# Last layer, first image: the nine convolution steps of both channel halves taken in turn on DVE

## The chip, the cores and the metric

The kernel runs on one core of a Trainium2 chip. The metric is the device time of one execution in microseconds, and the figure of a kernel is the median of several executions. Engine names are those of the profile: PE multiplies matrices (PEld loads its weights), DVE, ACT and POOL do elementwise work, SP issues the DMAs of this kernel. One core has one of each. The engines run at the same time; each takes its own instructions strictly in order, and semaphores make an instruction wait for another engine or for a DMA.

## The reference, cut to what matters

Four layers follow one another on a batch of 4 images of 192 channels and 56 x 56 pixels, all float32. The first three are an attention with a 7 x 7 convolution and an MLP, a channel attention, and a windowed attention with a gated MLP. The change is in the fourth, a scan in four directions:

```python
xn = _ln_cf(x, ln_w, ln_b)                             # layer norm over the channels
xz = jnp.einsum('dc,bchw->bdhw', in_proj_w, xn)
xc, z = jnp.split(xz, 2, axis=1)                       # 192 channels each
xc = jax.lax.conv_general_dilated(xc, conv_w, (1, 1), 'SAME', feature_group_count=xc.shape[1])
xc = jax.nn.silu(xc + conv_b[None, :, None, None])     # 3 x 3, each channel by itself
...
x_dbl = jnp.einsum('kcd,bkdl->bkcl', x_proj_w, xs)     # xs: xc by rows, by columns, and both reversed
dts, Bv, Cv = jnp.split(x_dbl, [R, R + N], axis=2)
dt = jax.nn.softplus(jnp.einsum('kdr,bkrl->bkdl', dt_proj_w, dts) + dt_proj_b[None, :, :, None])
ys = _selective_scan(xs, dt, A, Bv, Cv) + Ds[None, :, :, None] * xs
...                                                    # y: the sum of the four directions
y = _ln_cf(y, out_norm_w, out_norm_b) * jax.nn.silu(z)
return x + jnp.einsum('cd,bdhw->bchw', out_proj_w, y)
```

The selective scan is a recurrence along the pixels, h = exp(dt A) h + dt B u, for 192 channels with 4 states each, and its output is the sum of C h over the states.

## The kernel before

**Tiles.** The 192 channels lie as two halves (`h` = 0, 1) of 96 partitions. An image is worked through in 7 chunks of 8 image rows, 448 pixels (`NCHUNK`, `CH`). For each image `b` and chunk `c` the generator `begin(b, c)` does the front of the layer:

- a DMA brings the chunk's rows of x into a `row` tile; POOL clears the edges of a tile `pad` and copies the two rows above from the chunk before; two `pad` tiles are used in turn;
- `layer_norm`: PE means (L1823), DVE subtracts (L1825), ACT squares (L1833), PE takes the variance (L1838), ACT Ln and Exp (L1841, L1842), DVE multiplies (L1844). L1825, L1833 and L1844 handle both halves in one instruction of 896 elements;
- PE projects the two halves of the convolution's source (L1878, in `project`) and ACT writes them into `pad` (L1889, one instruction a half);
- the 3 x 3 convolution of each half, in nine steps, from `pad` into `u`. For image 0 the steps run on DVE: a `tensor_scalar` for the first tap with the bias (L1912), eight `scalar_tensor_tensor` (L1914) that each multiply a shifted view of `pad` by a weight and add `u`. For images 1 to 3 they are nine matrix multiplications on PE with diagonal weights (L1921), made once on DVE by `diagonals` (L1958);
- PE projects the halves of z (L1878 again) and ACT copies them out (L1939, into a `gate` tile);
- ACT takes SiLU of `u` (L1944) and of z (L1945), the latter goes to memory (`zmem`), and `product` multiplies `u` by the scan's projection (PE L1975, ACT L1978, a DMA to `prods`).

The convolution handles 7 image rows in chunk 0 (392 elements a step), 8 in chunks 1 to 5 (448), 9 in chunk 6 (504), because it lags the chunk by one row.

**The scan** follows in `load` (DMAs of the projected values: `dr`, `bc`), `sizes` (PE L2067, ACT softplus L2079, into `dt`), `decay` (DMAs that spread `dt` over the states into `da`, ACT exponential L2113) and `scan`: DVE forms `du` (L2128; L2131 for columns), PE repeats it for the states (L2138), DVE multiplies by B (L2144) and scans (L2160), POOL multiplies by C (L2167), PE sums over the states (L2183), DVE adds to `y` (L2188, L2197). Two directions start on an image's rows, then come its columns.

**The order of the work.** No engine's order is written by hand as a list. All work is in generators such as `begin`; before each group of instructions a generator yields what the group costs on a planning clock. The class `Order` keeps all open generators, works out for each when its next group could start (its engine's last planned end, the end of the group it depends on plus 0.25, free buffers), takes the earliest, with a small charge for a later place in the program (`HURRY` times the place), emits its instructions, and goes on. So the order of each engine's instructions is fixed when the program is built, and it depends on the costs that the generators yield:

```python
def on_dve(*n, takes=(), ready=None, each=0.00105):
    return "DVE", sum(0.08 + each * i for i in n), takes, None, ready
```

An optional `ready` replaces the end of the group before as the earliest start. `table=` names the set of functions that an ACT group needs; where it differs from the one last used, an ACT table load is emitted (L331) and 1.3 is charged.

**What stands around.** Image 0's front of the last layer is emitted among the end of the third layer and the start of the last layer's scan. Of the third layer the steps concerned are a norm of its last chunks (PE L1249, ACT L1260, L1268, L1269, DVE L1271), its depthwise convolution on DVE (L1397 and L1399, taps outside, the parts of a tap inside the loop), and the MLP's multiplications and their elementwise work (L1488, L1499, L1523, L1553, L1562, L1570, L1580). Two large clears by POOL (L2243) stand at the start of the scan.

Of the kernel before, what the change touches and what calls it, by code (L numbers as in the profile page):

```python
# [22 lines left out]
B, C, H, W = 4, 192, 56, 56  # L23
# [204 lines left out]
def pixels(ap):  # L228

    return ap.rearrange("(h p) n -> p h n", p=HALF)  # L230
# [9 lines left out]
def rows2(ap, w=W):  # L240
    return ap.rearrange("p (y x) -> p y x", x=w)


class Order:
# [29 lines left out]
    def take(self, kind="bank"):  # L274
        slot = min((s for s in self.kinds[kind] if s[0] is not None), key=lambda s: s[0])
        slot[0] = None
        return slot[1]

    def done(self, tile):

        (slot,) = (s for slots in self.kinds.values() for s in slots if s[1] is tile)
        slot[0] = self.end + self.LATENCY
# [57 lines left out]
def on_pe(n, *takes, ready=None):  # L340

    return "PE", 0.0019 * n, takes, None, ready


def on_dve(*n, takes=(), ready=None, each=0.00105):
    return "DVE", sum(0.08 + each * i for i in n), takes, None, ready
# [6 lines left out]
def on_act(*n, takes=(), table=None, ready=None):  # L353
    return "ACT", sum(0.2 + 0.0009 * i for i in n), takes, table, ready


def on_pool(*n, each=0.0011):
    return "POOL", sum(0.2 + each * i for i in n), (), None, None


def on_sp(*takes):
    return "SP", 0.5, takes, None, None
# [1371 lines left out]
def layer3(tc, order, pools, src, packs, aps, dst):  # L1734
# [80 lines left out]
    def gone(*what):  # L1815
        return what in passed

    def layer_norm(x, out, over=(), read=None):

        yield on_pe(2 * CH, "bank")  # L1820
        mean = take()
        for k in range(2):
            nc.tensor.matmul(mean[:HALF, :CH], ones, x[:, k], start=(k == 0), stop=(k == 1))  # L1823
        yield on_dve(2 * CH)
        nc.vector.tensor_sub(out[:HALF], x[:HALF], bcast(mean[:HALF, :CH], 1, 2))  # L1825
        done(mean)
        for t in over:
            done(t)
        if read:
            passed.add(read)  # L1830
        yield on_act(2 * CH, takes=("sq3",))
        sq = take("sq3")
        nc.scalar.activation(sq[:HALF], out[:HALF], AF.Square)  # L1833
        yield on_pe(2 * CH, "bank")
        vt = take()
        var = vt[:HALF, :CH]
        for k in range(2):
            nc.tensor.matmul(var, ones, sq[:, k], start=(k == 0), stop=(k == 1))  # L1838
        done(sq)
        yield on_act(CH, CH, table=EXP_LN)  # L1840
        nc.scalar.activation(var, var, AF.Ln, bias=eps)  # L1841
        nc.scalar.activation(var, var, AF.Exp, scale=-0.5)  # L1842
        yield on_dve(2 * CH)
        nc.vector.tensor_mul(out[:HALF], out[:HALF], bcast(var, 1, 2))  # L1844
        done(vt)

    def begin(b, c):

        yield lambda: (b, c) == (0, 0) or (gone("begun", b, c - 1) if c else gone("begun", b - 1, NCHUNK - 1))
        yield lambda: b < 2 or gone("scanned", b - 2)

        yield lambda: b == 0 or gone("multiplied", 8 * NSC * (b - 1) + 4 * c)

        yield lambda: order.at2["tail"] >= NCHUNK * (b + 1)
        u = us[b % 2]
        yield on_sp("row", "row")
        xl, xn = take("row"), take("row")
        nc.sync.dma_start(xl[:HALF], pixels(src[b])[:, :, c * CH : (c + 1) * CH])  # L1860

        i = NCHUNK * b + c
        pad, above = pads[i % 2], pads[(i - 1) % 2]
        yield lambda: i < 2 or gone("convolved", i - 2)
        yield on_pool(200, 200)
        nc.gpsimd.memset(pad[:HALF, :, :, 0 : W + 2 : W + 1], 0.0)
        if c == 0:
            nc.gpsimd.memset(pad[:HALF, :, 1], 0.0)
        else:
            nc.gpsimd.tensor_copy(pad[:HALF, :, 0:2, 1 : 1 + W], above[:HALF, :, 8:10, 1 : 1 + W])  # L1870
        if c == NCHUNK - 1:
            nc.gpsimd.memset(pad[:HALF, :, 10], 0.0)
        yield from layer_norm(xl, xn, over=(xl,))

        def project(m):
            px = take()
            for k in range(2):
                nc.tensor.matmul(  # L1878
                    px[:HALF, :CH], inT[:, k, HALF * m : HALF * m + HALF], xn[:, k], start=(k == 0), stop=(k == 1)
                )  # L1880
            return px

        tiles = []
        for m in range(2):
            yield on_pe(2 * CH, "bank")
            tiles.append(project(m))
        for m in range(2):
            yield on_act(CH)
            nc.scalar.activation(  # L1889
                pad[:HALF, m, 2:10, 1 : 1 + W],  # L1890
                rows2(tiles[m][:HALF, :CH]),
                AF.Identity,
                bias=in_b[:, m : m + 1],
            )
            done(tiles[m])
        passed.add(("begun", b, c))
        y0, y1 = max(8 * c - 1, 0), 8 * c + (8 if c == NCHUNK - 1 else 7)
        n = y1 - y0
        at = y0 - (8 * c - 1)
        px = slice(y0 * W, y1 * W)  # L1900
        zt = None
        for h in range(2):
            pz = pc = uh = None
            if b == 0:

                for t in range(9):
                    yield on_dve(n * W, each=0.0012, ready=order.end - 0.3 if t else None)
                    v = pad[:HALF, h, at + t // 3 : at + t // 3 + n, t % 3 : t % 3 + W]
                    uh = rows2(u[:HALF, h, px])
                    wt = w["c96.conv_w"][:, h, t : t + 1]  # L1910
                    if t == 0:
                        nc.vector.tensor_scalar(uh, v, wt, w["c96.conv_b"][:, h : h + 1], ALU.mult, ALU.add)  # L1912
                    else:
                        nc.vector.scalar_tensor_tensor(uh, v, wt, uh, ALU.mult, ALU.add)  # L1914
            if uh is None:
                yield lambda: gone("diagonals")
            for t in range(9 if uh is None else 0):
                yield on_pe(n * W, *(("bank",) if t == 0 else ()), ready=order.end - 0.5 if t else None)
                if t == 0:
                    pc = take()  # L1920
                nc.tensor.matmul(  # L1921
                    rows2(pc[:HALF, : n * W]),
                    diag[:, h, t],
                    pad[:, h, at + t // 3 : at + t // 3 + n, t % 3 : t % 3 + W],
                    start=(t == 0),
                    stop=(t == 8),
                )
            if uh is None:
                yield on_act(n * W)
                nc.scalar.activation(  # L1930
                    u[:HALF, h, px], pc[:HALF, : n * W], AF.Identity, bias=w["c96.conv_b"][:, h : h + 1]
                )
                done(pc)
            yield on_pe(2 * CH, "bank")
            pz = project(2 + h)
            yield on_act(CH, takes=() if h else ("gate",))
            if h == 0:
                zt = take("gate")
            nc.scalar.activation(zt[:, h], pz[:HALF, :CH], AF.Identity, bias=in_b[:, 2 + h : 3 + h])  # L1939
            done(pz)  # L1940
        done(xn)
        passed.add(("convolved", i))
        yield on_act(2 * n * W, 2 * CH, table=SILU)
        nc.scalar.activation(u[:HALF, :, px], u[:HALF, :, px], AF.Silu)  # L1944
        nc.scalar.activation(zt, zt, AF.Silu)  # L1945
        yield on_sp()
        nc.sync.dma_start(pixels(zmem[b])[:, :, c * CH : (c + 1) * CH], zt)
        done(zt)
        yield from product(b, 0, px, u[:, :, px], 2)
        passed.add(("rows", b, c))  # L1950
# [16 lines left out]
    def product(b, o, px, u, passes):  # L1967

        n = px.stop - px.start
        yield on_pe(passes * n, "bank")  # L1970
        pp = take()

        out = pp[:40, :n].rearrange("p (x y) -> p y x", y=H) if o else pp[:40, :n]
        for k in range(2):
            nc.tensor.matmul(out, w["c128.xpT"][:, k, o], u[:, k], start=(k == 0), stop=(k == 1))  # L1975
        yield on_act(n, takes=("prod",))
        t = take("prod")
        nc.scalar.copy(t[:, :n], pp[:40, :n])  # L1978
        done(pp)
        yield on_sp()  # L1980
        nc.sync.dma_start(prods[b][o][:, px], t[:, :n])
        done(t)
# [227 lines left out]
    n = 8 * NSC  # L2210
# [72 lines left out]
```

## Time and profile before

| | us |
|---|---|
| median of 3 executions | 6766.48 |
| lowest to highest | 6764.02 to 6773.46 |
| the profiled execution, its own time | 6756.62 |
| its span in the profile | 6754.8 |
| busy: PE, DVE, ACT, POOL | 5757.1, 5976.0, 2615.2, 1414.7 |
| mean granted PE clock | 0.931 of full speed |
| ACT table loads, 373 of 1283 ns | 478.6 |

The profile is of one execution. Its page gives the busy time of each engine, the span in 40 equal slices (of 169 us here), the groups of instructions by line, engine and tile with their mean durations and what ended the idle time before them, and the chain of work that ended last. Queries of the trace give the same for a stretch of time: busy time by stage, and a timeline, in which one row is one instruction or a run of like instructions on one engine (start, length, engine, line, operation, output<-inputs, shapes, count, then in brackets the idle time before it and the releaser). A row's length for a run of several instructions is from the first start to the last end. The front of image 0 in the last layer lies between 4789 and about 4980 us of the span.

### The profile page before, as it was taken

The page shows a single profiled execution, that of the slowest core. Times are in us where ns is not written, and L with a number is a line of the kernel's source. Part 1 is how long each engine was busy: PE and PEld are TensorE (multiplying, and loading weights), DVE is VectorE, ACT ScalarE, POOL GpSimd, SP SyncE. Part 2 cuts the span into 40 slices and gives each one's busy share as a digit, 9 for nine tenths or more (in the row PEclk, how much of TensorE's full clock was granted, in tenths as well). Part 3 has the DMA queues.
Part 4 walks back from the last instruction along what each step waited for, and adds up shares of the span by engine and source line. Part 5 has one row for each costly group of instructions (what it writes and reads, how often), then busy time and mean ns, then how long its engine had stood idle before and what let it go on. Part 6 is the DMA issues. An engine that isn't in the chain of part 4 may idle for free.

```text
span 6754.8 us, 107251 instructions
## 1 busy us (share of the span) xinstructions
PE 5757.1 (85%) x43558; PEld 2642.5 (39%) x43558; DVE 5976.0 (88%) x7515; ACT 2615.2 (39%) x4049; POOL 1414.7 (21%) x1413
## 2 busy tenths in 40 slices
PE   6999889999999995768888788786689889889776
PEld 3444444444444442335444444453222222222211
DVE  2999999999999999838999899898888887887997
ACT  1121121222222121125555455454366566566544
POOL 0000000000000000132222222221025544545564
PEclk9999889999999997889999899998799999999998
DMA  4222112221222112210000000000045555655654
GB/s 107 59 53 59 36 30 62 52 67 34 54 56 73 30 44 75 62 42 16 18 18 16 18 19 15 18 18 22 23 113 134 150 144 131 161 134 138 171 149 118
DMA packets 252042, 462.65 MB, mean 68 GB/s; under 512 B 30388, under 2 KB 237964, under 8 KB 240412
## 3 DMA queue, kind: packets, MB, share of 16 engines
q1 hardware_dynamic: 251548, 455.80, 26.8%
q8 instruction: 343, 5.62, 0.4%
q14 instruction: 151, 1.24, 0.1%
HBM read 238.58 MB, written 62.96 MB: 45 GB/s over the span
## 4 chain that ended last, share of the span: by engine, by line
DVE 26%; PE 20%; issue 4%; ACT 4%; POOL 1%; DMA 1%; SPq 0%; DVEq 0%; POOLq 0%; ACTq 0%
DVE bg L1399 6%; PE bank L1921 4%; DVE st L2160 3%; DVE bxn L1399 3%; PE bank L1878 2%; DVE bank L2144 2%; PE bank L2138 2%; PE bank L2183 2%; PE bank L1562 1%; PE bank L1265 1%; DVE bacc L1711 1%; PE bank L2011 1%; PE bank L1249 1%; DVE e L1650 1%; PE bank L1488 1%
## 5 line engine op out<-in xcount | busy, mean ns | idle before, releaser
L811 DVE TENSOR_TENSOR pr<-vdx,attn 112x1792 f32<-112x1792 f32 (+4 forms) x720 | 1185.9, 1648 | 19.2
L656 PE MATMUL bank<-qk_in,w_a 64*49 64x392 f32 x9408 | 1157.4, 496 | 0.0
L2167 POOL TENSOR_TENSOR da<-st,bc 128x448 f32<-128x448 f32 x672 | 857.3, 1281 | 844.2 <-DVE st L2160 630.3
L816 DVE TENSOR_TENSOR oa<-oa,pr 112x1792 f32<-112x1792 f32 (+1 forms) x423 | 765.0, 1808 | 0.0
L656 PE MATMUL bank<-qk_in,wd 64*49 64x392 f32 x4032 | 691.3, 494 | 0.0
L2160 DVE TENSOR_TENSOR_SCAN st<-da,st,bank 128x448 f32<-128x448 f32 x576 | 646.8, 1132 | 0.7 <-ACT da L2113 0.7
L656 PEld LDWEIGHTS bank<-qk_in,w_a 64*49 64x49 f32 x9408 | 431.7, 120 | 396.1 <-issue 390.4
L1147 POOL MEMSET bxl<- 128x1008 f32 x3 | 2.7, 938 | 2783.3 <-DVE ob L825 2783.3
L2144 DVE TENSOR_TENSOR bank<-bank,bc 128x448 f32<-128x448 f32 x672 | 382.7, 617 | 114.6 <-PE bank L2138 114.1
L331 ACT ACT_TABLE_LOAD x373 | 478.6, 1283 | 6.7
L2113 ACT ACTIVATE da<-da,a_neg 128x448 f32<-128x448 f32 x672 | 413.8, 658 | 111.7 <-DMA da<-dt 109.6
L1399 DVE SCALAR_TENSOR_TENSOR bg<-bzpad,w_b,bg 128x448 f32<-128x448 f32 (+2 forms) x672 | 423.6, 685 | 0.0
L2183 PE MATMUL bank<-da,w_c 128*32 128x448 f32 x1344 | 355.5, 575 | 72.7 <-POOL da L2167 66.9
L816 DVE TENSOR_TENSOR ob<-ob,pr 112x1792 f32<-112x1792 f32 (+3 forms) x282 | 393.1, 1394 | 0.0
L902 ACT ACTIVATE hm<-bank,w_a 128x448 f32<-128x448 f32 x168 | 106.4, 634 | 637.3 <-PE bank L893 617.8
L2138 PE MATMUL bank<-du,w_c 32*128 32x448 f32 x1344 | 261.6, 626 | 105.0 <-DVE du L2128 62.8
L656 PEld LDWEIGHTS bank<-qk_in,wd 64*49 64x49 f32 x4032 | 247.8, 119 | 256.7 <-issue 254.8
L893 PE MATMUL bank<-xc,w_a 128*128 128x448 f32 x672 | 296.8, 571 | 58.6 <-DVE xc L878 58.6
L608 ACT ACTIVATE qk_in<-bank,qk_bias,qk_scale 64x224 f32<-64x224 f32 (+5 forms) x288 | 146.3, 526 | 445.5 <-PE bank L593 443.2
L1488 PE MATMUL bank<-bxn,w_b 128*128 128x448 f32 (+2 forms) x672 | 291.4, 562 | 22.5 <-DVE bxn L1271 17.1
L908 PE MATMUL bank<-hm,w_a 128*96 128x448 f32 x672 | 288.5, 561 | 20.2 <-ACT hm L902 20.2
L1921 PE MATMUL bank<-pad,diag 128*96 128x448 f32 (+2 forms) x756 | 297.4, 543 | 2.3 <-ACT pad L1889 2.3
(309 smaller groups left out, 9908.4 us busy)
## 6 DMA issues: line engine op xcount, KB each, us to landing
da<-dt SPq DMA_DIRECT2D x672, 224.0 KB
vdx<-vmem SPq DMA_DIRECT2D x168, 476.0 KB
bc<-prod SPq DMA_DIRECT2D x224, 224.0 KB
row<-x SPq DMA_DIRECT2D x56, 336.0 KB
x<-x SPq DMA_DIRECT2D x4, 2352.0 KB
vmem<-vt SPq DMA_DIRECT2D x56, 168.0 KB
xc<-x SPq DMA_DIRECT2D x56, 168.0 KB
mid<-xc SPq DMA_DIRECT2D x56, 168.0 KB
```

What stands on the lines that cost most here:

```text
L331: self.nc.scalar.preload_act_table_set(table)
L656: nc.tensor.matmul(py[a][outs[g], : 7 * W].rearrange("p (y x) -> p y x", x=W), wt[halves[a], dx], q[halves[a], r, i0 + m : i0 + m + 7, dx ...
L811: nc.vector.tensor_mul(pr, vv, wt)
L816: nc.vector.tensor_add(og, og, before)
L1399: nc.vector.scalar_tensor_tensor(dst, x, wt[:, t : t + 1], dst, ALU.mult, ALU.add)
L1921: nc.tensor.matmul(rows2(pc[:HALF, : n * W]), diag[:, h, t], pad[:, h, at + t // 3 : at + t // 3 + n, t % 3 : t % 3 + W], start=(t == 0), ...
L2113: nc.scalar.activation(da, da, AF.Exp, scale=a_neg[:, k, g : g + 1])
L2138: nc.tensor.matmul(tiles[j][:, :SCH], w["c96.rep"][r], du[r], start=True, stop=True)
L2144: nc.vector.tensor_mul(tiles[j][:, :SCH], tiles[j][:, :SCH], b_)
L2160: nc.vector.tensor_tensor_scan(sts[j][:, r], da[:, r], tiles[j][:, :SCH][:, r], first, ALU.mult, ALU.add)
L2167: nc.gpsimd.tensor_mul(da, sts[j], c_)
L2183: nc.tensor.matmul(py[32 * j : 32 * j + 32, :SCH], w["c128.sum"], das[j], start=True, stop=True)
```

## The change

For image 0, the nine taps are now the outer loop and the two halves the inner one, both halves of a tap in one group. A group yields the cost of two steps with `on_dve`'s own 0.00105 an element (before: one step, 0.0012 an element), and its earliest start from the second tap on is the end of the last planned group less 0.1 (before: less 0.3). The z projections of both halves and their copies, which stood behind each half's convolution, now stand behind all 18 steps. For images 1 to 3 the emitted instructions are the same as before. Lines after the edit lie one lower for the steps themselves (L1911, L1913) and one higher below it.

```diff
         zt = None
-        for h in range(2):
-            pz = pc = uh = None
-            if b == 0:
-
-                for t in range(9):
-                    yield on_dve(n * W, each=0.0012, ready=order.end - 0.3 if t else None)
+        if b == 0:
+
+            for t in range(9):
+                yield on_dve(n * W, n * W, ready=order.end - 0.1 if t else None)
+                for h in range(2):
                     v = pad[:HALF, h, at + t // 3 : at + t // 3 + n, t % 3 : t % 3 + W]
                     uh = rows2(u[:HALF, h, px])
                     wt = w["c96.conv_w"][:, h, t : t + 1]
...
                         nc.vector.tensor_scalar(uh, v, wt, w["c96.conv_b"][:, h : h + 1], ALU.mult, ALU.add)
                     else:
                         nc.vector.scalar_tensor_tensor(uh, v, wt, uh, ALU.mult, ALU.add)
-            if uh is None:
-                yield lambda: gone("diagonals")
-            for t in range(9 if uh is None else 0):
+        else:
+            yield lambda: gone("diagonals")
+        for h in range(2):
+            pz = pc = None
+            for t in range(9 if b else 0):
                 yield on_pe(n * W, *(("bank",) if t == 0 else ()), ready=order.end - 0.5 if t else None)
...
-            if uh is None:
+            if b:
                 yield on_act(n * W)
```

## The prediction

> **What bounds the kernel now.** I read the page's 40 slices first: DVE at 8 or 9 tenths nearly everywhere, PE beside it. The edited steps stand in one place, so I then read busy time by stage. Columns: stage, its length, then busy us (instructions) of PE, PEld, DVE, ACT, POOL; granted clock; DMA share; GB/s.
>
> ```profile
> 4789.00:4857.00 68.00, 40.78 (x89) 15.70 (x87) 60.16 (x85) 28.86 (x37) 2.00 (x4) 0.81 0.06 17
> 4857.00:4980.00 123.00, 87.42 (x218) 31.87 (x218) 105.45 (x161) 68.11 (x92) 21.52 (x20) 0.87 0.32 85
> 4980.00:5091.00 111.00, 102.60 (x349) 33.28 (x350) 85.92 (x114) 67.60 (x97) 49.65 (x45) 0.96 0.54 135
> ```
>
> The convolution of image 0 lies in the first two rows. No engine is full there: in the second DVE idles 17.6 us of 123, PE 36. The third row is PE's. Why DVE idles shows in its timeline over chunk 2 (start, us, engine, line, tiles, count, idle before and its releaser):
>
> ```profile
> 4881.82 5.74 DVE L1914 SCALAR_TENSOR_TENSOR u<-pad,w_c,u 96x448 f32<-96x448 f32 x8
> 4887.48 1.07 DVE L1825 TENSOR_TENSOR row<-row,bank 96x896 f32<-96x896 f32 x1
> 4888.48 0.50 DVE L1912 TENSOR_SCALAR u<-pad,w_c 96x448 f32<-96x448 f32 x1
> 4889.01 5.70 DVE L1914 SCALAR_TENSOR_TENSOR u<-pad,w_c,u 96x448 f32<-96x448 f32 x8
> 4894.63 1.08 DVE L1844 TENSOR_TENSOR row<-row,bank 96x896 f32<-96x896 f32 x1
> 4898.64 0.51 DVE L1912 TENSOR_SCALAR u<-pad,w_c 96x448 f32<-96x448 f32 x1 [2.94 <-ACT pad L1889]
> ```
>
> L1825 and L1844 are the two DVE steps of the next chunk's layer norm. L1825 stands between the two halves, so ACT's and PE's part of that norm runs under the second half:
>
> ```profile
> 4888.59 0.95 ACT L1833 ACTIVATE sq<-row 96x896 f32<-96x896 f32 x1 [5.90 <-DVE row L1825]
> ...
> 4889.59 3.15 PE L1838 MATMUL bank<-sq,c_ones 128*96 128x448 f32 x4 [4.29 <-ACT sq L1833]
> ...
> 4892.78 0.60 ACT L1841 ACTIVATE bank<-bank,c_eps 96x448 f32<-96x448 f32 x1 [1.42 <-PE bank L1838]
> 4893.41 0.52 ACT L1842 ACTIVATE bank<-bank 96x448 f32<-96x448 f32 x1
> ...
> 4894.93 1.28 ACT L331 ACT_TABLE_LOAD   x1
> ...
> 4896.23 0.95 ACT L1944 ACTIVATE u<-u 96x896 f32<-96x896 f32 x1
> ...
> 4897.92 0.61 ACT L1889 ACTIVATE pad<-bank,in_b 96x448 f32<-96x448 f32 x1
> ```
>
> From L1825's start to L1842's end are 6.45 us, all but L1825's own 1.0 hidden by the 6.15 us of the second half. The stage ends on DVE: PE, dry, waits for a DVE step queued behind the last chunk's convolution.
>
> ```profile
> 4981.93 1.87 PE L2138 MATMUL bank<-du,w_c 32*128 32x448 f32 x6 [11.49 <-DVE du L2128]
> ```
>
> So a microsecond here counts in full, whichever engine loses it.
>
> **What the Trainium skill says.** "Perfetto Trace Analysis", section "DVE / Act Engine Instruction": a record runs from the start in the ALUs to the write's acknowledgement, and only that releases a semaphore, while a next instruction may begin to fetch earlier. The trace agrees: eight dependent L1914 of 448 elements start every 0.703 us (5.70 for eight, the last one's record 0.08 longer than its step), records of 0.681. "VectorE: DVE Perf Modes", "The DRAIN you can't avoid", says that a semaphore between DVE instructions costs nothing. The trace differs: L1399 in layer 2 does the same operation on two halves in turn and starts every 0.597 us:
>
> ```profile
> 4599.67 2.46 DVE L1399 SCALAR_TENSOR_TENSOR bxn<-bapad,w_b,bxn 96x448 f32<-96x448 f32 x4
> ```
>
> (2.46 less one record of 0.67, over three steps.) I take the trace. "ScalarE: Activation LUTs", "What ACT_TABLE_LOAD costs", gives 1283 ns; the page's row has 1283.
>
> **The change part by part.** Both built programs' orders of instructions can be compared without any time. No instruction is added; one of 373 table loads falls away (1.28 us of ACT, which has idle time here: nothing). On DVE the order differs from 4789 us to about 5091 us; the last 1823 DVE, 2332 PE, 1386 ACT, 707 POOL and 1178 SP instructions stand in the same order as before. So the difference is made in 300 us and carried to the end.
>
> *Removed:* the wait of a step for its predecessor. 7 chunks x 2 halves x 8 steps x (0.703 - 0.597) = 11.9 us of DVE, 1.7 a chunk. Bounds: 0 (the step stays 0.703) to 12.
>
> *Moved, at no cost:* the first half's z projection and its copy L1939 no longer come between the halves of the source, but on PE they stand ahead of L1838 and on ACT ahead of L1841, as before, under that norm's own waits. The lost table load is in the same place.
>
> *Moved:* L1825 of the next chunk now stands behind all 18 steps, and in chunks 1 to 3 L1844 directly behind it. Nothing is left to cover the norm, and L1844 waits at the head of DVE's queue; the taps of its chunk stand behind it, and PE's two projections into pad (L1878) and ACT's L1889 wait for it. A chunk then costs: first taps 0.6 (the second half's needs the second L1889, 0.6 later) + 0.45; 16 x 0.597 = 9.55; L1825's start to L1844's start 6.65 (6.45 and the hand-over; 5.65 of it idle); L1844 to the next first tap 4.5. The last is ACT's, in which the projections (two of L1878, 3.25 us in all with the load) are hidden: behind L1842 stand the second z copy L1939 0.63, a table load 1.28, L1944 0.87, L1945 0.85, L1889 0.63. Sum 21.75 us; before it was 18.87 (4879.77 to 4898.64).
>
> *Start:* the second first tap goes ahead of layer 2's last convolution (+0.5), and chunk 0's two SiLUs with their two table loads now precede L1268 on ACT, on which layer 2's last norm waits. ACT: L1260 ends 4829.7, L1939 0.63, load 1.28, 0.86, 0.93, load 1.28, L1268 and L1269 1.2: L1271 starts near 4835.9, before 4833.38. The 24 L1399 and chunk 1 behind them start 2.5 later.
>
> *Chunks 4 and 5:* here the scan's DVE steps fill. In chunk 4, 9 diagonal copies and a du lie in the gap (2 of 5.65 us), then 5.2 us of scan between L1844 and the taps; in chunk 5, 4.2 us and 3.1 us. Chunk 6 is pure convolution: 1.1 + 16 x 0.667 (504 elements, L1399's step) = 11.8 against 16.34, which held 2.2 us of scan steps.
>
> First taps, estimated, with the lag behind before in brackets. Chunk 1: 4860.0 (+2.5). Its last L1570 waits for PE as before; four of its steps and L1825 follow, L1825 at 4874.9, L1844 6.65 later, so chunk 2: 4886.0 (+6.3; before lost 1.5 there, its first tap taking 2.01 us beside POOL's memset, which is over by then). Chunk 3, 21.75 on: 4907.75 (+9.1). Chunk 4, as much again: 4929.5 (+11.0; before, two softplus copies and a table load held this one up). Chunk 5: 10.6 + 6.65 + L1844's 1.0 + 5.2 on: 4952.95 (+12.7). Chunk 6: 10.6 + 6.65 + 1.0 + 3.1 on: 4974.3 (+11.1). End: 4986.1 (+6.5).
>
> Then PE: L1825, L1833 and L1838 follow 6.9 us behind that end instead of 8.2 (1.6 us of multiplications and sums left over go first), and 22 us of PE in either kernel lead to the first L1921 of image 1: +5.2, with one L2067 (0.9) still to do. **+6 us.** SP's and POOL's queues: loads of da are issued one at a time between loads of dr and bc instead of six together; the first is issued some 11 us ahead of its use, where before at most 9.7 us sufficed, so I charge nothing; if late, see the first rival. POOL's pad copies follow L1889 as before.
>
> The profiled execution took 6756.62 us with a span of 6754.8, 9.9 under the median of the runs, 6766.48. Against its own time: 6762.6; on the median: 6772.5.
>
> **Rivals.** *Slower: the scan work that should fill chunks 4 and 5 is late.* DVE runs in order; a scan step there that waits for da (load, then L2113 on ACT) holds the convolution behind it. 12.5 us of such steps lie in these gaps; if landing plus L2113 take over about 11 us, most of it comes on top: +6 and up to 12, 6784. For: these queues are rebuilt just here. Against: 9.7 us sufficed.
> *Slower: it doesn't do what it says*: the step stays at 0.703. +6 + 11.9 = 6784. Against: 0.597 in L1399.
> *Faster: the gaps are cheaper.* L1838 took 3.15 to 3.30 us after PE had idled, but 1.74 in chunk 1; at 1.74, five chunks lose 7.5 less, and if PE's 8.4 idle us of the third stage also go, 6772 - 16 = 6756. Over 0.2% needs more: the full 11.9 without any open norm, or the clock after 5091: 1% of 1400 us of PE is 14 us, either way.
>
> **How the numbers follow.** 0.2% is 13.5 us, about what a measurement of this kernel can tell from no change. Forecast (a loss of 0 to 13): 0.53. Slower by more, the two slower rivals and gaps that I have under-priced: 0.36. Faster by more: 0.11. The likeliest is 6772; its own range 6764 to 6780. The range goes down to the cheap gaps, 6756, and up past the slower rivals, 6790.
>
> **What would show it.** Right: L1914's step near 0.60; before L1844 idle of 4 to 6 us on ACT L1842 in chunks 1 to 3, where there was none; a chunk of 21 to 22 us; the convolution's end 4 to 9 us later. Wrong: L1844 without idle before it, a chunk under 19 us, or a difference that arises after 5091.

## The result, and the profile after

Over 20 executions of each, the median went from 6761.88 to 6775.67 us. The ratio after to before is 1.0025 with a 95% interval of 1.0019 to 1.0031, that is 16.9 us (12.8 to 21.0) slower; the medians differ by 13.8. The number lies in the range (6756 to 6790), and the direction is the forecast one, but the loss was put at 6 us; by either figure it lies past the 13.5 us that had been called no difference, though the interval reaches a little below that. The profiled execution took 6769.90 us with a span of 6767.7.

The three stages again, now of the kernel after (columns as in the prediction):

```profile
4789.00:4857.00 68.00, 43.87 (x88) 16.74 (x86) 57.06 (x84) 28.48 (x37) 9.99 (x4) 0.81 0.06 16
4857.00:4980.00 123.00, 77.51 (x184) 29.82 (x186) 83.70 (x139) 53.33 (x73) 20.56 (x19) 0.76 0.26 69
4980.00:5091.00 111.00, 97.35 (x324) 31.35 (x320) 81.11 (x110) 64.36 (x94) 41.81 (x40) 0.94 0.49 122
```

In the second row DVE is busy for 83.70 us where it was 105.45. That is no saving: the row holds 139 DVE instructions instead of 161, and PE's busy time and granted clock (0.76, it was 0.87) fell with it. The work moved to the right. The DVE timeline over chunk 2 shows both halves of the forecast:

```profile
4886.94 1.09 DVE L1911 TENSOR_SCALAR u<-pad,w_c 96x448 f32<-96x448 f32 x2 [4.43 <-ACT pad L1889]
4887.95 9.61 DVE L1913 SCALAR_TENSOR_TENSOR u<-pad,w_c,u 96x448 f32<-96x448 f32 x16
4897.49 1.07 DVE L1825 TENSOR_TENSOR row<-row,bank 96x896 f32<-96x896 f32 x1
4904.12 1.08 DVE L1844 TENSOR_TENSOR row<-row,bank 96x896 f32<-96x896 f32 x1 [5.56 <-ACT bank L1842]
4910.26 1.09 DVE L1911 TENSOR_SCALAR u<-pad,w_c 96x448 f32<-96x448 f32 x2 [5.05 <-ACT pad L1889]
```

Sixteen taps take 9.61 us: less one record of 0.67 and over 15 steps, 0.596 us a step. Before it was 0.717 (the prediction's L1914 line at 4889.01: 5.70 us less one record of 0.68, over seven steps). And L1844 idles 5.56 us for ACT's L1842, where it had no idle before. The chunk takes 23.3 us (4886.94 to 4910.26) instead of 18.87 (which contained 1.5 us of a first tap slowed beside POOL's clear). What ACT and PE do in that gap (same columns):

```profile
4899.60 3.30 PE L1838 MATMUL bank<-sq,c_ones 128*96 128x448 f32 x4 [8.98 <-ACT sq L1833]
...
4902.69 6.18 PE L1878 MATMUL bank<-row,w_c 128*96 128x448 f32 x12
...
4903.57 0.52 ACT L1842 ACTIVATE bank<-bank 96x448 f32<-96x448 f32 x1
...
4905.90 0.63 ACT L1940 ACTIVATE gate<-bank,in_b 96x448 f32<-96x448 f32 x1 [1.81 <-PE bank L1878]
4906.55 1.28 ACT L331 ACT_TABLE_LOAD   x1
...
4909.54 1.14 ACT L1889 ACTIVATE pad<-bank,in_b 96x448 f32<-96x448 f32 x2
```

PE has stood idle for 8.98 us and then needs 3.30 us for L1838. (In the kernel before, L1838 is about as slow, 3.15 us in chunk 2, but the second half covers it.) The second z copy (L1940) waits 1.81 us for PE's projections, and all of ACT's queue, the two SiLUs (L1945, L1946) and L1889, on which the next taps wait, moves back with it. The trace also records the clock that PE was granted: 0.50 of full speed from 4899.60 to 4902.90 us.

Behind the convolution, PE in the kernel after:

```profile
4995.98 1.87 PE L2139 MATMUL bank<-du,w_c 32*128 32x448 f32 x6 [6.16 <-DVE du L2129]
4998.91 3.30 PE L1838 MATMUL bank<-sq,c_ones 128*96 128x448 f32 x4 [1.06 <-ACT sq L1833]
5002.14 1.72 PE L2184 MATMUL bank<-da,w_c 128*32 128x448 f32 x6
5003.78 1.46 PE L2139 MATMUL bank<-du,w_c 32*128 32x448 f32 x6
```

The same steps in the kernel before:

```profile
4987.84 1.82 PE L1838 MATMUL bank<-sq,c_ones 128*96 128x448 f32 x4
...
4991.41 1.03 PE L2138 MATMUL bank<-du,w_c 32*128 32x448 f32 x6
...
5003.01 0.95 PE L2183 MATMUL bank<-da,w_c 128*32 128x448 f32 x6
```

This slowness and the waits behind it were not in the sum.

**One clock for all kernels.** The time that passes before the edited place differs between the profiles by up to 17 us, so I count from the start of the last layer's first L1825, and take three marks from each trace: the end of the convolution; the start of the 49th scan (L2160), about where the orders of all these kernels have become the same again, here called the equal point; and the difference. "PE idle" is the time up to the equal point less PE's busy time in it. Where multiplications on constant data were added (e5, e10, e11) they count as busy. For e7 the first mark is the end of the chunks that stay on DVE.

| kernel | conv. end | behind it | equal point | PE idle | ratio of the runs to before (95%) |
|---|---|---|---|---|---|
| before | 226.1 | 115.4 | 341.5 | 78.5 | |
| after | 238.9 | 125.1 | 364.0 | 94.1 | 1.0025 (1.0019 to 1.0031) |
| e1 norm covered | 214.8 | 125.6 | 340.4 | 75.1 | 0.9999 (0.9991 to 1.0007) |
| e2 chained | 247.3 | 126.1 | 373.4 | 103.4 | 1.0040 (1.0027 to 1.0052) |
| e3 costs only | 228.4 | 114.6 | 343.0 | 77.2 | 0.9997 (0.9989 to 1.0006) |
| e4 norm ahead | 223.3 | 124.5 | 347.8 | 76.5 | 0.9996 (0.9987 to 1.0004) |
| e5 PE busy | 229.1 | 125.1 | 354.2 | 56.9 | 1.0013 (1.0005 to 1.0021) |
| e6 deep | 235.2 | 118.9 | 354.1 | 88.3 | 1.0015 (1.0009 to 1.0022) |
| e7 PE conv. | 158.5 | 198.6 | 357.1 | 61.9 | 1.0019 (1.0010 to 1.0028) |
| e9 z first | 234.7 | 119.7 | 354.4 | 81.8 | 1.0010 (0.9999 to 1.0020) |
| e10 covered, PE busy | 216.7 | 124.3 | 341.0 | 57.8 | 0.9993 (0.9985 to 1.0001) |
| e11 PE busy behind | 229.0 | 127.6 | 356.6 | 50.5 | 1.0025 (1.0016 to 1.0034) |
| e12 scan in place | 224.7 | 119.7 | 344.4 | 76.2 | 0.9995 (0.9987 to 1.0003) |

A second profile of the kernel after (e8) gave 238.9, 125.1 and 364.1, so, as far as one repeat can tell, a difference of 1 us in these marks means something. The loss of 22.5 us at the equal point is 12.8 in the convolution and 9.7 behind it. Seen from PE, it is 15.6 us more idle time (94.1 instead of 78.5) and 6.9 us more busy time (269.9 instead of 263.0) for the same matmuls: PE's granted clock up to that point was 0.85 of full speed instead of 0.89.

### The profile page after: what moved, and what is told of

The parts are those of the page before. It is cut to its first block, busy times and chain, and to the rows that moved or that the text cites. A ratio compares the mean times of both kernels' runs of the same rounds, so it can differ in the third digit from the quotient of the medians.

```text
span 6767.7 us, 107254 instructions
## 1 busy us (share of the span) xinstructions
PE 5757.2 (85%) x43558; PEld 2644.8 (39%) x43558; DVE 5964.9 (88%) x7515; ACT 2613.6 (39%) x4048; POOL 1433.3 (21%) x1413
## 3 DMA queue, kind: packets, MB, share of 16 engines
q8 instruction: 343, 5.62, 0.4%
## 4 chain that ended last, share of the span: by engine, by line
DVE 26%; PE 20%; ACT 4%; issue 4%; DMA 1%; POOL 1%; SPq 0%; DVEq 0%; POOLq 0%; ACTq 0%
DVE bg L1399 6%; PE bank L1922 4%; DVE st L2161 3%; DVE bxn L1399 3%; PE bank L1878 2%; DVE bank L2145 2%; PE bank L2139 2%; PE bank L2184 2%; PE bank L1562 1%; PE bank L1265 1%; PE bank L1249 1%; DMA da<-dt 1%; DVE bacc L1711 1%; PE bank L2012 1%; ACT L331 1%
## 5 line engine op out<-in xcount | busy, mean ns | idle before, releaser
L2145 DVE TENSOR_TENSOR bank<-bank,bc 128x448 f32<-128x448 f32 x672 | 382.4, 617 | 107.3 <-PE bank L2139 106.5
L1399 DVE SCALAR_TENSOR_TENSOR bg<-bzpad,w_b,bg 128x448 f32<-128x448 f32 (+2 forms) x672 | 423.6, 686 | 0.0
L2184 PE MATMUL bank<-da,w_c 128*32 128x448 f32 x1344 | 355.5, 572 | 71.9 <-POOL da L2168 65.9
L2139 PE MATMUL bank<-du,w_c 32*128 32x448 f32 x1344 | 257.7, 619 | 103.4 <-DVE du L2129 59.8
```

The source lines that it names most:

```text
L1399: nc.vector.scalar_tensor_tensor(dst, x, wt[:, t : t + 1], dst, ALU.mult, ALU.add)
L2139: nc.tensor.matmul(tiles[j][:, :SCH], w["c96.rep"][r], du[r], start=True, stop=True)
L2145: nc.vector.tensor_mul(tiles[j][:, :SCH], tiles[j][:, :SCH], b_)
L2184: nc.tensor.matmul(py[32 * j : 32 * j + 32, :SCH], w["c128.sum"], das[j], start=True, stop=True)
```

## The experiments

**e1: cover the norm again, keep the halves in turn.** L1825 passes a mark, and the fifth tap waits in the order for the next chunk's mark.

```diff
             for t in range(9):
+                if t == 4 and c < NCHUNK - 1:
+                    yield lambda: gone("centred", b, c + 1)
                 yield on_dve(n * W, n * W, ready=order.end - 0.1 if t else None)
```

> The halves in turn as in the kernel after, but before the fifth tap of a chunk the order waits until the next chunk's L1825 has been emitted, so 10 steps (5.97 us at 0.597) cover the rest of that chunk's norm (5.65 us). Theory 1 (the exposed norm is the loss, the shorter step the gain): no idle before L1844 in chunks 1 to 3, a chunk of about 17.1 us (10.6 taps, 2.0 for the two norm steps, 4.5 to the next tap), the convolution's end some 8 to 12 us before that of the kernel before; time 6752 (6746 to 6758). Rival (the planner's costs, or the changed order behind the convolution, make the loss): 6768 to 6780, like the kernel after.

The DVE timeline of e1 (L1917 the taps, L1846 the norm's second step):

```profile
4902.19 1.07 DVE L1825 TENSOR_TENSOR row<-row,bank 96x896 f32<-96x896 f32 x1
4903.18 6.04 DVE L1917 SCALAR_TENSOR_TENSOR u<-pad,w_c,u 96x448 f32<-96x448 f32 x10
4909.14 1.08 DVE L1846 TENSOR_TENSOR row<-row,bank 96x896 f32<-96x896 f32 x1
4914.82 0.51 DVE L1915 TENSOR_SCALAR u<-pad,w_c 96x448 f32<-96x448 f32 x1 [4.60 <-ACT pad L1891]
```

L1846 has no idle, and the convolution ends 24.1 us ahead of the kernel after and 11.3 ahead of the kernel before, as theory 1 said. The time did not follow: the ratio is 0.9999, a median of 6764.06 us where 6752 was expected. Behind the convolution e1 needs 125.6 us and not 115.4. Counting instructions up to the convolution's end shows a part of the reason (e12 measures it): 12 matmuls of L2138 instead of 18, 6 of L2183 instead of 12 (the program's; the profile has two records of each), and 3 scans instead of 6. A scan half-step that used to run under the slower convolution is left over. So the exposed norm makes the loss of the kernel after (23.6 us at the equal point), and all the rest of the change, the shorter step with it, is worth 1.1 us there.

**e2: keep the order of the kernel after, chain the taps again.** In the same 18 places, nine of half 0, then nine of half 1.

```diff
-                for h in range(2):
+                for h, q in (divmod(2 * t, 9), divmod(2 * t + 1, 9)):
```

> The order and the planner's costs of the kernel after, but each half's nine taps follow one another again (nine of half 0, then nine of half 1, in the same 18 places). Theory 1: the step is 0.70 again, 1.7 us a chunk, and L1844 still waits 5.6 us: the kernel after plus 8 to 12: 6786 (6782 to 6790). Rival (the step's length is hidden by what the chunk waits for): as the kernel after, 6776.

```profile
4927.66 5.70 DVE L1913 SCALAR_TENSOR_TENSOR u<-pad,w_c,u 96x448 f32<-96x448 f32 x8
```

Eight chained steps take 5.70 us in e2's timeline, as in the kernel before. The convolution ends 8.4 us later than in the kernel after, the equal point lies 9.4 later, the ratio is 1.0040. So with the norm exposed the step counts, but not in full: 8.4 us of the 13.5 that 112 steps of 0.121 each add up to. Nothing arrives from chunk 0 (the first tap of chunk 1 starts 106.1 us in with either order), and behind chunks 1 and 2 a part goes into a shorter wait from L1844 to the next tap (4.98 and 4.94 us instead of 5.51 and 6.14).

**e3: the planner's two numbers alone.** The kernel before, with the change's cost and earliest start.

```diff
-                    yield on_dve(n * W, each=0.0012, ready=order.end - 0.3 if t else None)
+                    yield on_dve(n * W, ready=order.end - 0.1 if t else None)
```

> The kernel before with only the two planner's numbers of the change (0.00105 an element and the end less 0.1), halves one after the other. Theory 1: L1825 still stands between the halves, 6762 within 6. Rival (the planner's numbers make the loss): 6770 to 6780.

0.9997, and 1.5 us at the equal point. The planner's numbers alone cost nothing; what is left of the change is the new order of the halves, without the break between them.

**e4: pull the norm further ahead.** As e1, with the next chunk's L1825 behind the first tap and its L1844 behind the seventh.

```diff
+                if t == 1 and c < NCHUNK - 1:
+                    yield lambda: gone("centred", b, c + 1)
+                if t == 7 and c < NCHUNK - 1:
+                    yield lambda: gone("normed", b, c + 1)
```

> The halves in turn, and the next chunk's norm pulled further ahead: its L1825 stands behind the first tap, its L1844 behind the seventh, so four steps also cover the projections and L1889. Theory 1: no idle before L1844 nor most of that before the first tap; a chunk of 13 to 15 us; time 6738 (6728 to 6750). Rival (the SiLUs ahead of L1889 on ACT, or the first scan steps, are the next bound): as the covered version, 6748 to 6756.

```profile
4904.21 7.95 PE L1881 MATMUL bank<-row,w_c 128*96 128x448 f32 x16 [4.54 <-DVE row L1846]
...
4909.72 0.62 ACT L1892 ACTIVATE pad<-bank,in_b 96x448 f32<-96x448 f32 x1
...
4910.45 0.51 DVE L1918 TENSOR_SCALAR u<-pad,w_c 96x448 f32<-96x448 f32 x1 [3.91 <-ACT pad L1892]
```

A miss: the idle moved from the norm to the first tap. All four projections of a chunk stand in one row on PE behind L1846, 7.95 us, and ACT's writes into `pad` wait for them. The ratio, 0.9996, is that of e1.

**e5: keep PE busy while it waits for ACT's square.** The kernel after, with multiplications on constant data into the bank that L1838 overwrites.

```diff
         var = vt[:HALF, :CH]
+        for _ in range(warm):
+            nc.tensor.matmul(vt[:HALF, :384], ones, inT[:, 0], start=True, stop=True)
...
-        yield from layer_norm(xl, xn, over=(xl,))
+        yield from layer_norm(xl, xn, over=(xl,), warm=12 if b == 0 and c >= 2 else 0)
```

> The kernel after, with 12 matrix multiplications of 384 columns on constant data ahead of each L1838 of image 0 from chunk 2 on; they write the bank that L1838 then overwrites, while PE waits for ACT's square anyway. Theory A (a PE that has idled runs L1838 at half speed, 3.30 us, and that is part of the exposed norm): L1838 takes 1.74 us, the idle before L1844 falls from 5.6 to about 4.0 us, five times, and the multiplications behind the convolution start warm: 6767 (6762 to 6771). Rival (the speed of PE there is hidden or does not follow from idleness): 6774 to 6780.

The groups of L1838 in the convolution's stretch, first in the kernel after, then in e5, where that line is L1840 (columns: busy us, mean ns of one, idle before it and its releaser):

```profile
L1838 PE MATMUL bank<-sq,c_ones 128*96 128x448 f32 x20 | 16.4, 974 | 42.2 <-ACT sq L1833 42.2
```

```profile
L1840 PE MATMUL bank<-sq,c_ones 128*96 128x448 f32 x20 | 8.6, 551 | 3.0 <-ACT sq L1833 3.0
```

And DVE's timeline in e5:

```profile
4920.23 1.07 DVE L1825 TENSOR_TENSOR row<-row,bank 96x896 f32<-96x896 f32 x1
4925.31 1.08 DVE L1846 TENSOR_TENSOR row<-row,bank 96x896 f32<-96x896 f32 x1 [4.01 <-ACT bank L1844]
4929.99 1.16 DVE L1913 TENSOR_SCALAR u<-pad,w_c 96x448 f32<-96x448 f32 x2 [3.59 <-ACT pad L1891]
```

The instruction takes 551 ns instead of 974, the idle before the norm's second step is 4.0 instead of 5.6 us, and from there to the next tap 4.7 us instead of the 5.5, 6.1 and 4.7 of the kernel after in chunks 1 to 3. Convolution and equal point come 9.8 us earlier and the ratio falls from 1.0025 to 1.0013. The order of the kernel's own instructions is that of the kernel after, and PE's granted clock from 4875 to 4985 us is 1.00, where the kernel after has 0.81 from 4880 to 4992. So of the 22.5 us at the equal point some 10 are PE at half speed because it had been idle. "TensorE: Matmul & The Clock Gate" in the Trainium skill, Part 1 ("The HAM clock gate"), says that PE's clock falls to half after an idle window of about 3.4 us and comes back after as long a busy one; the pair here, 974 ns after long idle against 551 kept busy, agrees.

**e6: a deeper pipeline.** As e4, with the z projections ahead of the taps and the SiLUs behind the next chunk's L1889.

```diff
+        for h in range(2 if b == 0 else 0):
+            yield on_pe(2 * CH, "bank")
+            pz = project(2 + h)
...
+        yield lambda: b > 0 or c == NCHUNK - 1 or gone("begun", b, c + 1)
         yield on_act(2 * n * W, 2 * CH, table=SILU)
```

> The halves in turn; the z projections of a chunk ahead of its taps; the next chunk's L1825 behind the first tap and its L1844 behind the seventh; the SiLUs of a chunk behind the next chunk's L1889. Theory B (up to the point where the orders are the same again, about 340 us behind the first norm, PE has some 240 us to do, so only PE's idle time counts, and a shorter convolution is worth what it takes off that): chunks 1 to 3 of 13 to 14 us instead of 17.6, the convolution's end 15 to 25 us before that of the kernel before, but scan steps are left over for behind it: 6752 (6740 to 6760). Rival C (what the convolution saves on DVE arrives in full): 6738 to 6745.

```profile
4931.28 1.08 DVE L1825 TENSOR_TENSOR row<-row,bank 96x896 f32<-96x896 f32 x1 [4.23 <-PE bank L1823]
```

A miss, and slower than the kernel before (1.0015): now DVE waits in the middle of the taps for the next chunk's means (L1823), which PE reaches late behind the four projections.

**e7: chunks 4 to 6 of image 0's convolution on PE.** As e1, with the diagonals made one chunk earlier.

```diff
-        if b == 0:
+        if i < 4:
...
-            for t in range(9 if b else 0):
+            for t in range(9 if i >= 4 else 0):
...
-            if b:
+            if i >= 4:
```

> The covered version with the convolution of image 0's chunks 4 to 6 on PE, as for images 1 to 3: 33 us off DVE, 21 us of L1926 onto PE. Theory B: PE's idle time falls by what it does meanwhile, about as much as it gets to do: 6758 (6750 to 6766). Rival C (DVE's steps are the limit): 6730 to 6740.

1.0019. The 33 us taken from DVE brought nothing: PE is busy 32.2 us longer up to the equal point (357.1 less 61.9 of idle, against 341.5 less 78.5) and idle 16.6 less, and the difference is the 15.6 us that the point lies later. Theory B had the limit right (PE, not DVE) and the trade wrong: PE got more work than its idle time shrank by.

**e8: the kernel after once more**, with no edit.

> The kernel after, unchanged, for a second profile. Behind the point where the orders are the same again the first profile won back 9 us of the 22.6 that it lay behind. If that comes from idle PE time before (a higher granted clock later), the second profile shows it too (6 to 10 us); if it is the spread of the clock from run to run, anything from -8 to +10.

The marks repeat to 0.1 us. From the equal point to the end the two profiles took 1646.6 and 1643.4 us, before 1655.6. But e3, whose order is nearly that of before, took 1664.2 there, and over all profiles PE's busy time for the same 4629 records of matmuls ran from 1381 us (e8) to 1408 (e3). That goes with the granted clock, 0.96 of full speed in this stretch of e8 and 0.93 in e3, and its spread is larger than the 9 to 12 us in question.

**e9: z projections first, norm covered.** e1 with this part of e6's edit:

```diff
+        for h in range(2 if b == 0 else 0):
+            yield on_pe(2 * CH, "bank")
+            pz = project(2 + h)
...
+            if b == 0:
+                continue
             yield on_pe(2 * CH, "bank")
             pz = project(2 + h)
```

> The covered version (e1) with the two z projections of a chunk and their copies ahead of its taps, so that after L1844 PE has only the two projections into pad to do before DVE can go on. Theory B (what counts is where PE stands at the point of equal order, 340.4 us behind the first norm in e1 and 341.5 in the kernel before): L1844 to the next tap 3.5 to 4.5 us instead of 5.7, the convolution some 6 to 10 us shorter, and the scan steps that stand earlier are done before its end: 334 at that point, 6755 (6748 to 6762). Rival (scan steps are left over again, as in e1): 340, 6763.

A miss: 354.4 at the equal point, where 334 was expected. Here the opposite of e1 happens: 8 scans and 24 L2138 are inside the convolution's stretch, which becomes 19.9 us longer than in e1, and only 5.9 us come back behind it.

**e10: e1 with PE kept busy**, by e5's multiplications.

```diff
+        yield from layer_norm(xl, xn, over=(xl,), mark=("centred", b, c), warm=8 if b == 0 and c >= 2 else 0)
```

> The covered version (e1) with 8 multiplications on constant data ahead of each L1838 of image 0 from chunk 2 on. Theory A (PE's half speed after idling is part of each chunk): L1844 to the next tap 4.6 instead of 5.7 us, five chunks: 335 at the point of equal order instead of 340.4; 6757 (6751 to 6762). Rival: nothing to gain, since the norm is covered: 340 and 6763.

341.0 at the equal point: no gain over e1 (340.4). L1838's own speed is hidden there, but this run can't say that PE's speed is worth nothing under cover: the added multiplications (5.40 us) outlast ACT's square, so L1844 comes 7.90 and 7.83 us behind L1825 in two chunks where e1 has 6.96 and 6.95, and PE cools again while it waits for L1844 (a granted clock of 0.73 in the projections from 4893.70 to 4900.10 us). The ratio of 0.9993 (0.9985 to 1.0001) is the lowest of all, but it can't be told from 1.

**e11: keep PE busy behind the convolution too.** e5 with 8 multiplications ahead of L1838 of image 1's first chunk and 10 ahead of the first L2139 behind the convolution.

```diff
+        for _ in range(10 if (t, h) == (1, 1) else 0):
+            nc.tensor.matmul(tiles[0][:HALF, :384], ones, inT[:, 0], start=True, stop=True)
         for j in range(3):
             r = slice(32 * j, 32 * j + 32)
```

> As e5 (the kernel after with PE kept busy ahead of L1838), and also 8 such multiplications ahead of L1838 of image 1's first chunk and 10 ahead of the first scan repeat behind the convolution (L2138 before, L2139 after), where PE stood idle for 6.16 us. In the kernel after, the stretch from the convolution's end to the point of equal order took 125.1 us, 9.7 more than before: 3.4 of it PE busy longer on the same instructions, 6.3 PE idle. Theory A (the 3.4 are half speed after that idle stretch): 121 to 122 us there, 350.5 at the point of equal order instead of 354.2 in e5; 6764 (6758 to 6768). Rival (the order alone makes the 9.7): 125 there, as e5.

```profile
4990.06 1.03 PE L2143 MATMUL bank<-du,w_c 32*128 32x448 f32 x6
4991.01 5.40 PE L1838 MATMUL bank<-w_c,c_ones 128*96 128x384 f32 x16
4996.25 1.67 PE L1840 MATMUL bank<-sq,c_ones 128*96 128x448 f32 x4
```

A miss in the time (350.5 was expected at the equal point). The instructions behind do run at speed (L1840 1.67 us instead of 3.30, six L2143 1.03 instead of 1.87), but the added 5.40 us stand on the path (L1840 starts 10.6 us behind the convolution's end, where L1838 started 6.84 behind it in the kernel after), and later ones are slower (the kernel's own matmuls take 109.4 us behind the convolution, 110.5 in the kernel after, 106.9 before). The equal point comes 2.4 us later than in e5. That half speed follows the idle stretch is shown; what it is worth behind the convolution is not.

**e12: e1 with the scan's first half-steps at their old place.**

```diff
+                if t == 0 and c in {4: 0, 5: 1, 6: 2}:
+                    yield lambda: gone("multiplied", {4: 0, 5: 1, 6: 2}[c])
```

> The covered version (e1), and the first three scan half-steps are held at the place that they have before: the taps of chunks 4, 5 and 6 are emitted behind L2138 of half-steps 0, 1 and 2, so that 6 scans (L2160 before) stand ahead of the convolution's end as before, and not 3 as in e1. Theory B (e1's gain of 11 us at the convolution's end was lost to a scan half-step left over, 6 multiplications of L2138 and 6 of L2183 and 3 scans, in the stretch behind): the convolution ends 3 to 6 us later than in e1, the stretch behind takes 115 to 118 instead of 125.6, the point of equal order at 333 to 337 (e1 340.4, before 341.5); 6755 (6749 to 6761). Rival D (those 10 us behind come from something else, or the scan steps stall DVE in the convolution by as much): 340 or later, 6763.

```profile
4922.68 1.08 DVE L1825 TENSOR_TENSOR row<-row,bank 96x896 f32<-96x896 f32 x1 [9.06 <-PE bank L1823]
4925.78 0.62 DVE L2135 TENSOR_TENSOR du<-dt,u 96x448 f32<-96x448 f32 x1 [2.03 <-ACT dt L2086]
```

The stretch behind falls to 119.7, so 5.9 of the 10.2 us that e1 lost there are the scan half-step left over; of the other 4.3, 3.7 are PE's busy time (110.6 us, before 106.9 on nearly the same work). But the convolution ends 9.9 us later than in e1. In the lines, DVE stands 9.06 us for PE's means of the next norm (L1823), where e1 stood 6.21 for L1891, and then 2.03 us for `dt`, which the scan's first step needs. The equal point is 344.4, and rival D holds. That the 11 us of e1 are worth nothing because the next work comes at PE's and ACT's pace is my reading of this; no run shows it alone.

## Why the prediction was right or wrong, point by point

- **The step** was right, 0.596 us against 0.597, but its saving was under-sized. The prediction took the old step to be 0.703 us because it read the last of eight records as longer than a step; the record (0.68) is shorter, and the step is 0.717. So a step saves 0.121 us, with 392, 448 and 504 elements alike, and all of them 13.5 us instead of 11.9.
- **The exposed norm** was right to 0.1 us: L1825 to L1844 6.69, 6.63 and 6.63 behind chunks 1 to 3 (predicted 6.65), idle 5.62, 5.56 and 5.56. e1 shows that this is the loss.
- **L1844 to the next first tap, "4.5"** was the first step to fail: 5.51, 6.14 and 4.72 us behind chunks 1 to 3. I took the gap for ACT's and the projections for hidden. PE, cold after its idle stretch, was late, and ACT's z copy waited for it (1.81 us in the lines above). With PE kept busy (e5) the step is 4.6 to 4.7. The prediction knew the two prices of L1838 (3.15 and 1.74) and used them for that instruction only, not for the projections behind it.
- **Chunks 4 and 5** were under-priced too: from L1844 to the next tap 8.09 us where 6.2 was charged in chunk 4, 4.68 where 4.1 in chunk 5. With PE kept busy they are 7.06 and 4.25, so PE's speed is a part of it. With the step above, the convolution's end came 12.4 us later on the profile's clock (12.8 on the one used here), not 6.5.
- **"+5.2" at image 1's first L1921, and "22 us of PE in either kernel"** was the second step to fail. L1838 did follow 6.84 us behind the end, as worked out (6.9), but from there to the first L1921 it took 26.4 us: L1838, six L2184 and six L2139 alone cost 2.7 more than before, at PE's half speed. The lag there was 15.7 us, not 5.2.
- **"One L2067 still to do"** failed too: between there and the equal point the lag grew by another 6.8 us. The sum treated that stretch as PE's with no new waits; PE's idle time behind the convolution went from 8.7 to 15.0 us.
- **The slower rivals.** The step did not stay at 0.703. Nor did DVE stand for scan data in the gaps: one idle of 0.94 us before L2145. Their 6784 was not reached for their reasons.
- **The faster rival** (gaps that are cheaper with a faster L1838) named the right lever but counted on it to come by itself; the change works against it, since PE is idle longer than before (94.1 us instead of 78.5) and at a lower granted clock. The 7.5 us that it put on that compare with e5's 9.8.
- **"Carried to the end"** held within the clock's spread: 22.5 us at the equal point, 13.6 at the end of the profile, 16.9 by the runs. In six of the seven kernels that were 12 us or more behind at the equal point, the ratio is worth less than the lag (e2: 27 of 31.9; e5: 9 of 12.7). But three that were within 3 us of the kernel before there come out lower as well (e3: 1.5 behind, 2.0 faster in the runs; e10: 0.5 ahead, 4.7 faster; e12: 2.9 behind, 3.4 faster). So this is no sign that idle PE time is paid back later by a higher granted clock; that stays open.
- **Luck.** That the median of 6775.67 lies near the 6772 forecast owes something to chance: the forecast started from 6766.48, the median of three executions, and twenty gave 6761.88. The loss itself was forecast as 6 us and was 13.8 to 16.9. It belongs to the outcome "slower by more", which had 0.36, and to the one of its three reasons that named under-priced gaps.

## What to carry to other kernels

Two halves interleaved on one engine shorten each step, but they also remove the break between the halves, and what used to slip in there (here one instruction of the next chunk's norm) may have been what kept three other engines working. When an edit lengthens a wait of PE, price not only the wait but the work behind it at the speed that PE has after idling; here that was some 10 of 22.5 us. And count a gain where the orders of the kernels meet again, not at the end of the stage that got shorter: e1 ended the convolution 11.3 us earlier than the old kernel and was 1.1 us ahead where the orders met.

## What the runs showed of the hardware that was not expected

A `tensor_scalar` on DVE waits for a POOL clear that runs beside it, while steps with two tensor inputs do not wait for it. In e1, DVE's first taps of chunk 2 and POOL's second large clear:

```profile
4894.09 4.60 DVE L1915 TENSOR_SCALAR u<-pad,w_c 96x448 f32<-96x448 f32 x2 [4.60 <-ACT pad L1891]
```

```profile
4892.59 5.32 POOL L2248 MEMSET u<- 32x6272 f32 x1
```

The pair takes 4.60 us where it takes 1.09 in the kernel after. The first tap alone takes 4.07 us and ends 0.25 us after the clear (4898.16 and 4897.91). The same 0.25 us lies between the two ends in every kernel whose first tap met this clear, the kernel before among them (2.01 us, ended at 4881.78, the clear at 4881.53). But six L1914 beside the first large clear of the kernel before took their usual 0.68 us.

The other way round, POOL's copy into `pad`, 0.37 us in most places, took 8.72 us in the kernel after (from 4848.50) while DVE ran its L1399 steps without a break, and ended 0.23 us after the last of them. In the kernel before, the same copy beside the same steps took 0.45 us, and one step 0.91 instead of 0.80.

"GPSIMD Engine Reference" in the Trainium skill, section "1. Specifications", says that the two engines share their access to the on-chip memory, with contention for DVE instructions in a two-port mode or with two inputs there. The copy agrees. For two inputs the clear does not: L1914 has two and was not held. Whether the first tap runs in a two-port mode no run shows; it has a faster pace for some sizes (0.51 us for 448 elements, 0.67 for 392). In e1 the clear held DVE 3.5 us longer than the kernel after was held, so its gain at the convolution's end stands after that cost.
